# A four-layer convolution stack with state-space scan: group norms through a product, and logarithms written to PSUM

## The chip, the cores and the metric

The kernel runs on one core of a Trainium2 chip. A core has five engines with a queue each: TensorE (PE, with its weight loads shown as PEld), VectorE (DVE), ScalarE (ACT), GpSimd (POOL) and SyncE (SP), which here issues nearly all transfers. Each queue runs in order: an instruction that waits holds back everything behind it on its engine. The metric is the device time of one execution in microseconds (us), lower is better. Before the change it is 4212.91 us, the median of three runs (4212.07 to 4213.04).

## The reference: what is computed

Four images of 128 channels and 64 x 64 pixels (4096 positions) go through four layers. Each layer first normalises its input over groups (32 groups of 4 channels each) and adds its result to that input:

```
gn(v): per image and group of 4 channels:  (v - mean) / sqrt(var + 1e-5)
x = x + attention(gn(x))      # one head over 4096 positions, 128 channels, softmax
x = x + conv5x5(gn(x))        # weights built from radial tables
x = x + ssm(gn(x))            # 1x1 product, causal conv of 4 taps, silu; delta = softplus(...);
                              # 64 channels forward, 64 backward, 64 states each:
                              # h = exp(delta*A)*h + delta*x*B ; y = sum over states of h*C + D*x ; 1x1 product
x = x + conv3x3(gn(x))        # the offset branch of the reference has no effect on the result
```

A group's mean and variance are over 4 channels times 4096 positions, so they need a sum over positions (along a partition) and one over channels (across partitions).

## The kernel before, in words

Channels lie on the 128 partitions, positions along them. An image's positions are cut into 8 blocks of 512 (`MM`) and 4 chunks of 1024 (`CH`).

**The scan is the backbone.** `scan_core` walks 1024 ticks: 256 for each image (4 chunks, 2 directions, 16 sets of 4 states, 2 halves of the channels). A tick `i` has these steps, each on its engine:
- drive (POOL, L1502): `db = dx * br` for tick i+2, one of three buffers;
- decay (ACT, L1495): `da = exp(de * a)` for tick i+1, in PSUM;
- recur (DVE, L1512): the scan `h = da*h + db`, and for most ticks the product with the row `cr` (L1515) behind it;
- weigh (POOL, L1533): that product for the other ticks (`to_pool`);
- collect (PE, L1551): sums over states, eight products for every two ticks of a set, issued three ticks behind;
- keep (ACT, L1528): the last column, for the next chunk.

Rows are loaded from DRAM by SP for each tick. While images wait in other stages PSUM is cut "wide" (a decay of 1024 in one instruction, two buffers); while the operands of the next image are made it is "narrow" (two decays of 512, three buffers, and a bank for the product's use). `widen` makes the turn between two ticks.

**All else is background work.** `images()` is a chain of Python generators that issue the attention, the 5x5 convolution (`conv_pairs`), the scan's operands (`scan_prep`, `scan_operands`) of the next image, and the last 3x3 convolutions (`conv`, `conv_last`) of earlier ones. Every `yield` names a cost, and twice in each tick the main loop takes work until a credit, half a `pace` of `PACES`, is used up. So a yield is no wait on the chip: it sets how much is issued between two ticks' own instructions, and so the order in every queue. At an image's boundary `before(b)` issues background work without ticks until the next image's first operands are ready. Image 0's first three layers run before the scan begins, with nothing beside them; the last convolution of image 3 runs after it ends.

**Group norms.** In a layer's last step each block's sum comes out of the instruction that writes the block (`st.sum`), and ACT squares the block less one of its pixels with an accumulator (`Sums.squares`, L338). `group_norm` then makes scale and offset. For these sums it runs 13 small DVE instructions: `aggregate` (L345 to L348), a transpose within blocks of 32 that brings four channels beside each other (L366), means and variances of groups (L374 to L384), and a transpose back (L386). Then it waits, in the order of work, for the next tick, and POOL takes the power -1/2 and the offset (L391, L392). ACT applies them (`normalise`, L397). There are four such norms with bn_stats before the attentions (tag a, not changed), and twelve with sums: e before the 5x5 convolution, s before the scan's operands, m before the last convolution, one of each for each image.

**Attention's end.** For image 1 and later the last half block is evicted from PSUM (L736), inverted (DVE, L744), divided (ACT, L753), turned to channels (PE, L758 and L763), added (ACT, L768) and squared (L338), with yields between these steps.

**The operand stage.** `scan_operands` works in slots: for each block taps on PE, halves and tanh on ACT (L1270, L1277), silu on DVE (L1281), products on PE, and softplus as max(z, 0) + log(1 + exp(-|z|)). The logarithms come in two groups of four blocks (L1343)[...]; `join` adds each to `delta` (L1318), for the first group on POOL and for the second on DVE; `drives` multiplies on POOL (L1323).

Of the kernel before, what the change touches and what calls it, by code (L numbers as in the profile page):

```python
# [24 lines left out]
F32 = mybir.dt.float32  # L25
I32 = mybir.dt.int32
AF = mybir.ActivationFunctionType
# [5 lines left out]
P = 128  # L33
# [13 lines left out]
PACES = 2.65, 2.62, 2.62, 1.55  # L47
# [6 lines left out]
def conv_preact_kernel(  # L54
# [72 lines left out]
    gsz = C // GROUPS  # L127

# [191 lines left out]
    class Sums:  # L320
# [12 lines left out]
        def squares(self, i, x, pixel):  # L333
            if not self.begun:
                nc.scalar.activation(self.away, pixel, AF.Identity, scale=-1.0)
                self.begun = True
# [5 lines left out]
        def aggregate(self):  # L342

            total = gn_sums[:, 0, 0:2]
            nc.vector.tensor_reduce(total, self.sums, AX.X, ALU.add)  # L345
            nc.vector.tensor_scalar(gcols[:, :, 0], total, 1.0 / L, None, ALU.mult)
            nc.vector.tensor_tensor(self.away, gcols[:, 0, 0:1], self.away, ALU.add)
            nc.vector.scalar_tensor_tensor(  # L348
                gcols[:, 1, 0:1], self.away, self.away, gcols[:, 1, 0:1], ALU.mult, ALU.subtract
            )  # L350
# [3 lines left out]
    def group_norm(st, name):  # L354
# [5 lines left out]
        by_sums = isinstance(st, Sums)  # L360
        if by_sums:
            st.aggregate()
        else:
            nc.vector.bn_aggr(gcols[:, :, 0], st.rearrange("p a b -> p (a b)"))
# [15 lines left out]
        nc.vector.tensor_tensor(means, means, vars_, ALU.subtract if by_sums else ALU.add)  # L380
# [7 lines left out]
        begun = ticks_begun[0]  # L388
        while begun and ticks_begun[0] == begun:
            yield 0.4  # L390
# [98 lines left out]
    def attention_first(b, xs, xn, v, st, loads):  # L489
# [112 lines left out]
        def settle(blk):  # L602
# [6 lines left out]
            st.squares(blk, xs[:, cut], xs[:, 0:1])  # L609
# [50 lines left out]
    def attention(b, xs, xn, v, st, safe, loads):  # L660
# [94 lines left out]
        def turn(blk):  # L755
# [6 lines left out]
            for t in range(TPM):  # L762
# [6 lines left out]
                xs[:, cut], sums.pop(blk), AF.Identity, bias=bv_c, accum_out=st.sum(blk)  # L769
# [3 lines left out]
        def squares(blk):  # L773
            st.squares(blk, xs[:, bass.ts(blk, MM)], xs[:, 0:1])
# [51 lines left out]
        yield HOP / 2  # L826
        invert(done)
        divide(done)
        yield HOP
        turn(NM - 1)  # L830
        yield 2 * PRODUCT
        squares(NM - 1)
        ready.add((b, "attended"))


    def conv(b, xs, tag, st, weights, k, finish, name, residual=False):
# [10 lines left out]
        gn = yield from group_norm(st, f"{name}{b}")  # L847
# [46 lines left out]
    def conv_last(b, xs, st, finish):  # L894
# [5 lines left out]
        gn = yield from group_norm(st, f"m{b}")  # L900
# [98 lines left out]
    def conv_pairs(b, xs, tag, st, st2, lean):  # L999
# [9 lines left out]
        gn = yield from group_norm(st, f"e{b}")  # L1009
# [89 lines left out]
        def add(c, y, acc):  # L1099
# [5 lines left out]
            st2.squares(i, chunk(xs, c, y), xs[:, 0:1])  # L1105
# [97 lines left out]
        yield HOP  # L1203
        done()
        ready.update({(b, "convolved"), "narrow"})
        while "wide" in pools:
            yield HOP
# [4 lines left out]
    def scan_prep(b, xs, st, mats4):  # L1212
# [3 lines left out]
        pad = KC - 1  # L1216
# [705 lines left out]
```

## Time and profile before

| what | value |
|---|---|
| median of three runs | 4212.91 us |
| the profiled execution, and its span | 4214.73 us, 4212.9 us |
| DVE busy | 3581.9 us (85%), 2561 instructions |
| POOL busy | 3519.0 us (84%), 1679 instructions |
| PE busy | 3684.3 us (87%), ends modelled |
| ACT busy | 2334.0 us (55%) |
| mean granted TensorE clock | 0.931 |
| first drive of the scan, end of the scan | about 674 us, about 4144 us |
| a tick beside an attention | about 3.15 us |
| a tick in an operand stage | about 5 us |

The page gives, for each engine, busy time as a share of the span; a group of instructions has its line, engine and operation, the tensors it writes and reads, its count, its busy time, the mean of one, and the idle time in front of it with what ended that. A timeline row has its start and duration in us and, in brackets, the idle time of its engine before it. Ticks are numbered here by their drive (the instruction that writes `db`), 0 to 1023.

### The profile page before, as it was taken

How to read it: one execution, taken by the hardware profiler on the slowest of the kernel's cores; microseconds unless marked ns; L12 is line 12 of the kernel's file. 1: busy time of each engine (PE TensorE's matmuls, PEld its weight loads, DVE VectorE, ACT ScalarE, POOL GpSimd, SP SyncE). 2: the span in 40 equal slices, each digit the busy share in tenths (PEclk: the TensorE clock that was granted, in tenths of full speed). 3: DMA queues.
4: the chain of work that ended last, by engine and by line, in shares of the span. 5: the costliest groups of instructions: out<-in, count | busy, mean ns of one | idle time of the engine just before them, and what ended most of it. 6: DMA issues, size and time to landing. Idle time of an engine off the chain costs nothing. (4 is left out here: it accounts for less than half of the span.)

```text
span 4212.9 us, 49863 instructions
## 1 busy us (share of the span) xinstructions
PE 3684.3 (87%) x17628; PEld 2132.3 (51%) x17628; DVE 3581.9 (85%) x2561; ACT 2334.0 (55%) x3911; POOL 3519.0 (84%) x1679
## 2 busy tenths in 40 slices
PE   8999997999998979999989789999898476575766
PEld 4444443888884327887853268888633122121212
DVE  3842216999999989999999889999999899999995
ACT  3344316667674376776654666676645554545442
POOL 2533315999999978999999889999998899999995
PEclk9999999999999989999999989999999688786877
DMA  2120006555555566555555665555555666666561
GB/s 65 40 94 26 3 20 241 192 195 186 195 187 193 190 243 214 196 193 193 193 185 191 212 233 194 190 191 196 189 185 205 247 198 221 207 209 236 193 236 58
DMA packets 223728, 740.99 MB, mean 176 GB/s; under 512 B 29662, under 2 KB 30942, under 8 KB 223212
## 3 DMA queue, kind: packets, MB, share of 16 engines
q1 hardware_dynamic: 221548, 736.99, 51.8%
q8 instruction: 140, 2.29, 0.2%
q14 instruction: 120, 0.98, 0.1%
q10 hardware_dynamic: 1920, 0.73, 0.1%
HBM read 662.14 MB, written 75.47 MB: 175 GB/s over the span
## 5 line engine op out<-in xcount | busy, mean ns | idle before, releaser
L1502 POOL TENSOR_TENSOR db<-dx,br 128x1024 f32<-128x1024 f32 x1024 | 2400.5, 2368 | 133.6 <-DVE hc L1512 38.9
L1495 ACT ACTIVATE da<-de,a_neg 128x1024 f32<-128x1024 f32 (+1 forms) x1092 | 1161.7, 1065 | 400.4 <-DVE hc L1515 269.4
L1512 DVE TENSOR_TENSOR_SCAN da<-da,last,db 128x1024 f32<-128x1024 f32 (+1 forms) x501 | 1151.1, 2298 | 13.0 <-ACT da L1495 5.8
L1515 DVE TENSOR_TENSOR hc<-da,cr 128x1024 f32<-128x1024 f32 (+1 forms) x714 | 834.1, 1168 | 62.7 <-issue 0.9
L1551 PE MATMUL y<-hc,sel 128*32 128x512 f32 x4096 | 605.5, 653 | 268.1 <-POOL hc L1533 178.3
L1533 POOL TENSOR_TENSOR hc<-hc,cr 128x1024 f32<-128x1024 f32 x348 | 823.2, 2366 | 14.4 <-ACT last L1528 11.9
L700 PE MATMUL sc<-r,x 128*128 128x256 f32 x3072 | 803.6, 387 | 29.4 <-ACT last L1528 16.5
L721 PEld LDWEIGHTS acc<-v,exchange 128*128 128x128 f32 x6144 | 800.2, 192 | 46.5 <-issue 10.0
L721 PE MATMUL acc<-v,exchange 128*128 128x129 f32 x6144 | 803.5, 275 | 0.0
L700 PEld LDWEIGHTS sc<-r,x 128*128 128x128 f32 x3072 | 530.9, 192 | 191.9 <-ACT last L1528 69.9
L1512 DVE TENSOR_TENSOR_SCAN hc<-da,last,db 128x1024 f32<-128x1024 f32 (+1 forms) x267 | 596.0, 2232 | 0.9 <-ACT da L1495 0.9
L713 ACT ACTIVATE exchange<-sc 128x512 f32<-128x512 f32 x768 | 444.7, 589 | 216.8 <-PE sc L700 209.0
L1551 PEld LDWEIGHTS y<-hc,sel 128*32 128x32 f32 x4096 | 114.0, 113 | 623.0 <-POOL hc L1533 252.4
L1512 DVE TENSOR_TENSOR_SCAN da<-da,db 128x1024 f32<-128x1024 f32 (+1 forms) x175 | 381.4, 2179 | 24.4 <-ACT da L1495 17.2
L522 POOL TENSOR_TENSOR sidep<-sidep,exchange 128x512 f32<-128x512 f32 x120 | 172.5, 1437 | 245.4 <-ACT exchange L504 242.9
L1528 ACT COPY last<-da 128x1 f32<-128x1 f32 x516 | 81.1, 157 | 510.8 <-DVE hc L1515 510.0
L504 ACT ACTIVATE exchange<-sc 128x512 f32<-128x512 f32 x256 | 152.6, 596 | 253.7 <-PE sc L503 248.9
L522 DVE TENSOR_TENSOR sided<-sided,exchange 128x512 f32<-128x512 f32 x120 | 98.7, 822 | 211.4 <-ACT exchange L504 210.4
L510 PE MATMUL acc<-exchange,v 128*128 128x512 f32 x512 | 262.0, 594 | 0.9
L503 PE MATMUL sc<-r,x 128*128 128x512 f32 x512 | 262.0, 594 | 0.6 <-ACT r L486 0.6
L865 PE MATMUL pcm<-xpm,cs 128*128 128x512 f32 x432 | 214.3, 645 | 42.6 <-ACT xpm L397 42.6
L1512 DVE TENSOR_TENSOR_SCAN hc<-da,db 128x1024 f32<-128x1024 f32 (+1 forms) x81 | 181.4, 2240 | 1.6 <-ACT da L1495 1.4
(266 smaller groups left out, 3094.6 us busy)
## 6 DMA issues: line engine op xcount, KB each, us to landing
br<-bm SPq DMA_DIRECT2D x512, 512.0 KB, 3.9
cr<-cm SPq DMA_DIRECT2D x512, 512.0 KB, 4.5
dx<-dxd SPq DMA_DIRECT2D x64, 512.0 KB, 5.8
de<-dd SPq DMA_DIRECT2D x64, 512.0 KB, 6.0
xs<-in_x_dram SPq DMA_DIRECT2D x16, 512.0 KB, 6.2
xsd<-xs SPq DMA_DIRECT2D x16, 512.0 KB, 5.6
xcd<-xc SPq DMA_DIRECT2D x16, 512.0 KB, 2.7
bm<-bs SPq DMA_DIRECT2D x32, 256.0 KB, 4.1
```

The source lines that it names most:

```text
L503: nc.tensor.matmul(sc, xn[:, bass.ts(j, P)], rq[blk], start=True, stop=True)
L510: nc.tensor.matmul(acc[blk], v[:, j, :C], ring[:, u % NRING, :], start=j == 0, stop=j == NJT - 1)
L522: eng.tensor_tensor(s, s, ring[:, u % NRING, :], ALU.add)
L700: nc.tensor.matmul(sc[:, bass.ts(n, HM)], xn[:, bass.ts(2 * k + n, P)], rq[blk][:, cut], start=True, stop=True,)
L713: nc.scalar.activation(pt, sc, AF.Exp)
L721: nc.tensor.matmul(acc[part][:, bass.ts(t, CV)], ring[:, u % NRING, n * HM + t * P : n * HM + (t + 1) * P], v[:, 2 * k + n, :], start=(k, ...
L1495: nc.scalar.activation(da, rep["de", b, c, d, g][:, bass.ts(h, size)], AF.Exp, scale=a_neg[:, at(i)])
L1502: nc.gpsimd.tensor_tensor(dbs[i], rep["dx", b, c, d, g], rows["b", b, c, d, q], ALU.mult)
L1512: nc.vector.tensor_tensor_scan(h, da, db[:, cut], before, ALU.mult, ALU.add)
L1515: nc.vector.tensor_tensor(hc[:, cut], h, rows["c", b, c, d, q][:, cut], ALU.mult)
L1533: nc.gpsimd.tensor_tensor(hcs[i], hcs[i], rows["c", b, c, d, q], ALU.mult)
L1551: nc.tensor.matmul(y[r : r + SG, :], sel, hcs[first + gg][:, bass.ts(h, MM)], start=False, stop=q == NQ - 1, tile_position=(0, r), skip_gr ...
```

## The change

- **The norm's mean over channels** is made by PE. A constant matrix `gmean` has 1/(4 x 4096) within each group of four channels and zero elsewhere; it is made once from the identity by two DVE instructions. `Sums.settle` reduces the block sums to two numbers a channel, multiplies them by `gmean` into two columns of a PSUM bank that its caller has at hand (`spare`), and makes variance and negative mean with four small DVE instructions that read PSUM. POOL's power and offset stay. `group_norm` is kept for the norms before the attentions.
- **The pixel** that is taken off before squaring becomes the group's mean of that pixel, by a one-column product (e and m); the s norm takes the e norm's mean (`follow`).
- **The order of work.** The norm's POOL steps follow in the tick of the norm; the wait for the next tick is now in front of the e norm (`next_tick` after the attention's last squares) and inside the s norm (`wait`). The yields between the steps of the attention's end are gone, as is the one before the last add of the 5x5 convolution for images 1 to 3. `scan_prep` no longer waits for the wide PSUM tiles to go before its norm, but after its first two blocks.
- **Logarithms.** For images 1 to 3, the first three of the second group are written to PSUM banks ("a", "z", "s2"); the fourth stays in SBUF, and its add goes to POOL.
- **Paces** are 2.60, 2.57, 2.57 instead of 2.65, 2.62, 2.62; the last stays 1.55.

```diff
-PACES = 2.65, 2.62, 2.62, 1.55
+PACES = 2.60, 2.57, 2.57, 1.55
+    gmean = const.tile([P, P], F32, name="gmean")
+    gpick = const.tile([P, GROUPS], F32, name="gpick")
+    nc.vector.tensor_reduce(
+        gpick, ident.rearrange("p (g s) -> p g s", s=gsz), AX.X, ALU.add
+    )
+    nc.vector.tensor_scalar(
+        gmean.rearrange("p (g s) -> p g s", s=gsz),
+        gpick.unsqueeze(2).to_broadcast([P, GROUPS, gsz]), 1.0 / (gsz * L), None, ALU.mult,
+    )
...
-        def squares(self, i, x, pixel):
+        def squares(self, i, x, pixel, spare):
+
+            self.spare = spare
             if not self.begun:
-                nc.scalar.activation(self.away, pixel, AF.Identity, scale=-1.0)
+                nc.tensor.matmul(spare[:, 0:1], gmean, pixel, start=True, stop=True)
+                nc.scalar.activation(self.away, spare[:, 0:1], AF.Identity, scale=-float(L))
                 self.begun = True
...
+        def follow(self, other):
+
+            self.away, self.begun = other.minus, True
+
+        def settle(self, name, wait=False):
...
+            total = small.tile([P, 2], F32, tag="gn_total", name=f"total_{name}")
             nc.vector.tensor_reduce(total, self.sums, AX.X, ALU.add)
...
+            mean, power = self.spare[:, 0:1], self.spare[:, 1:2]
+            nc.tensor.matmul(self.spare[:, 0:2], gmean, total, start=True, stop=True)
...
+            nc.vector.tensor_scalar(off, mean, self.away, -1.0, ALU.add, ALU.mult)
+            nc.vector.scalar_tensor_tensor(less, mean, self.away, off, ALU.add, ALU.mult)
+            nc.vector.scalar_tensor_tensor(var, less, GN_EPS, power, ALU.add, ALU.add)
+            nc.vector.tensor_scalar(minus, mean, -1.0, None, ALU.mult)
+            if wait:
+                yield from next_tick()
+            nc.gpsimd.tensor_tensor(rs, var, mhalf, ALU.pow)
+            nc.gpsimd.tensor_tensor(nb, minus, rs, ALU.mult)
+            return rs, nb
+
+    def next_tick():
+
+        begun = ticks_begun[0]
+        while begun and ticks_begun[0] == begun:
+            yield 0.4
...
         def squares(blk):
-            st.squares(blk, xs[:, bass.ts(blk, MM)], xs[:, 0:1])
+            spare = sums.pop(blk)
+            if blk + 1 == NM:
+                spare = slots.take("sp")
+            st.squares(blk, xs[:, bass.ts(blk, MM)], xs[:, 0:1], spare)
...
         evict(done)
-        yield HOP / 2
         invert(done)
         divide(done)
-        yield HOP
         turn(NM - 1)
-        yield 2 * PRODUCT
         squares(NM - 1)
+        yield from next_tick()
         ready.add((b, "attended"))
...
-        gn = yield from group_norm(st, f"e{b}")
+        gn = yield from st.settle(f"e{b}")
+        st2.follow(st)
...
-        yield HOP
+        if not lean:
+            yield HOP
         done()
         ready.update({(b, "convolved"), "narrow"})
-        while "wide" in pools:
-            yield HOP
...
+        gn = yield from st.settle(f"s{b}", True)
         xn = pools["big"].tile([P, VSIZE], F32, tag="V", name=f"xn2_{b}")
         nc.gpsimd.memset(xn[:, :pad], 0.0)
         nc.gpsimd.memset(xn[:, pad + L : 2 * pad + L], 0.0)
-        gn = yield from group_norm(st, f"s{b}")
...
         piece(0)
         piece(NM - 1)
-        yield HOP
+        while "wide" in pools:
+            yield HOP
...
-                eng = nc.vector if b > 0 and c >= NCH // 2 else nc.gpsimd
+                eng = nc.vector if b > 0 and NM // 2 <= i < NM - 1 else nc.gpsimd
                 eng.tensor_tensor(delta[:, cut], delta[:, cut], us.pop(i), ALU.add)
...
             for n in range(i, j):
-                nc.scalar.activation(us[n], us[n], AF.Ln)
+                to = us[n]
+                if b > 0 and j == NM and n - i < 3:
+                    to = bank(("a", "z", "s2")[n - i], f"ln_{b}_{n}")
+                nc.scalar.activation(to, us[n], AF.Ln)
+                us[n] = to
```

More of the change, by code (lines that the diff above doesn't have):

```diff
@@ L340, in squares, with cell @@
             )
[L342 to L350, printed above, removed]
+        def follow(self, other):
+            self.away, self.begun = other.minus, True
+        def settle(self, name, wait=False):
+            def cell(tag):
+                return small.tile([P, 1], F32, tag=f"gn_{tag}", name=f"{tag}_{name}")
+            total = small.tile([P, 2], F32, tag="gn_total", name=f"total_{name}")
+            nc.vector.tensor_reduce(total, self.sums, AX.X, ALU.add)
+            mean, power = self.spare[:, 0:1], self.spare[:, 1:2]
+            nc.tensor.matmul(self.spare[:, 0:2], gmean, total, start=True, stop=True)
+            off, less, var, rs, nb = (cell(tag) for tag in ("off", "less", "var", "rs", "nb"))
+            minus = self.minus = small.tile([P, 1], F32, tag=f"gn_mi{name[0]}", name=f"mi_{name}")
+            nc.vector.tensor_scalar(off, mean, self.away, -1.0, ALU.add, ALU.mult)
[11 more added lines that the diff above has]
+            yield 0.4
     junk = const.tile([P, MM], mybir.dt.bfloat16, name="junk")
@@ L358, in tile @@
             return small.tile([P, *shape], F32, tag=f"gn_{tag}", name=f"{tag}_{name}")
[L360 to L364, printed above, removed]
+        nc.vector.bn_aggr(gcols[:, :, 0], st.rearrange("p a b -> p (a b)"))
         turned, after = gn_work[:, 0], gn_work[:, 1]
@@ L379, in group_norm @@
         nc.vector.tensor_tensor(means, means, means, ALU.mult)
-        nc.vector.tensor_tensor(means, means, vars_, ALU.subtract if by_sums else ALU.add)
+        nc.vector.tensor_tensor(means, means, vars_, ALU.add)
         total = gn_sums[:, 1]
@@ L387, in group_norm @@
         rs, nb = tile("rs", 1), tile("nb", 1)
-        begun = ticks_begun[0]
-        while begun and ticks_begun[0] == begun:
-            yield 0.4
         nc.gpsimd.tensor_tensor(rs, back[:, 0, 0:1], mhalf, ALU.pow)
@@ L608, in settle @@
             )
-            st.squares(blk, xs[:, cut], xs[:, 0:1])
+            st.squares(blk, xs[:, cut], xs[:, 0:1], pb)
         rq[0] = queries(b, 0, xn, slots)
@@ L768, in turn @@
             nc.scalar.activation(
-                xs[:, cut], sums.pop(blk), AF.Identity, bias=bv_c, accum_out=st.sum(blk)
+                xs[:, cut], sums[blk], AF.Identity, bias=bv_c, accum_out=st.sum(blk)
             )
@@ L846, in conv @@
         nc.gpsimd.memset(xp[:, pad : hp - pad, wp - pad :], 0.0)
-        gn = yield from group_norm(st, f"{name}{b}")
+        gn = yield from st.settle(f"{name}{b}")
         xh = xs.rearrange("p (h w) -> p h w", w=W)
@@ L899, in conv_last @@
         nc.gpsimd.memset(rows[:, H + 1, :], 0.0)
-        gn = yield from group_norm(st, f"m{b}")
+        gn = yield from st.settle(f"m{b}")
         xh = xs.rearrange("p (h w) -> p h w", w=W)
@@ L1104, in add @@
             )
-            st2.squares(i, chunk(xs, c, y), xs[:, 0:1])
+            st2.squares(i, chunk(xs, c, y), None, acc)
         def advance(c):
@@ L1633, in scan_end @@
             yield PRODUCT
-            st.squares(i, xs[:, cut], xs[:, i * MM : i * MM + 1])
+            st.squares(i, xs[:, cut], xs[:, i * MM : i * MM + 1], po)
     def program(safe):
```

## The prediction

> **What bounds the kernel now.** I read the page first, then the windows of time, the timelines of the group norms and of the end of an operand stage, the groups, and last the end of the chain.
>
> Windows: stretch, its length, then busy us (and count) of PE, PEld, DVE, ACT, POOL, then PE clock, DMA share, GB/s. The first lies in an attention, the second in an operand stage, the third in the last scan.
>
> ```profile
> 680.00:1280.00 600.00, 581.41 (x3944) 468.00 (x3941) 569.60 (x344) 419.59 (x755) 580.64 (x254) 0.99 0.59 197
> 1468.00:1593.00 125.00, 89.55 (x358) 35.20 (x351) 106.16 (x113) 88.70 (x149) 97.64 (x49) 0.84 0.70 242
> 3920.00:4140.00 220.00, 144.16 (x443) 41.38 (x446) 215.57 (x118) 96.63 (x117) 216.52 (x94) 0.77 0.61 207
> ```
>
> Outside the operand stages GpSimd (POOL) and VectorE (DVE) are both full. Per three ticks POOL has three drives and one weighing, 4 x 2.32 = 9.28 us, and DVE 3.5 + 3.5 + 2.3 = 9.3: a tick is 3.1 us, and neither engine has more than the buffered drives, some two ticks, in hand. Whatever stands idle on either here is paid. The operand stage is different: 24 ticks in 123 us, with no engine full.
>
> Next the group norm of image 2 before its last convolution (DVE, then POOL):
>
> ```profile
> 3886.06 2.34 DVE L1512 TENSOR_TENSOR_SCAN hc<-da,last,db 128x1024 f32<-128x1024 f32 x1
> 3889.06 0.17 DVE L345 TENSOR_REDUCE gn_sums<-su_m 128x2 f32<-128x16 f32 x1 [0.66 <-ACT junk L338]
> 3889.27 5.00 DVE L346 TENSOR_SCALAR gcols<-gn_sums 128x2 f32<-128x2 f32 x1
> ...
> 3896.58 0.25 DVE L386 STREAM_TRANSPOSE back_m<-gn_work 128x64 f32<-128x64 f32 x1
> 3896.75 2.32 DVE L1512 TENSOR_TENSOR_SCAN da<-da,last,db 128x1024 f32<-128x1024 f32 x1
> ```
> ```profile
> 3891.90 2.34 POOL L1533 TENSOR_TENSOR hc<-hc,cr 128x1024 f32<-128x1024 f32 x1
> 3896.91 0.55 POOL L391 TENSOR_TENSOR rs_m<-back_m,mhalf 128x1 f32<-128x1 f32 x1 [2.66 <-DVE back_m L386]
> 3897.54 0.19 POOL L392 TENSOR_TENSOR nb_m<-back_m,rs_m 128x1 f32<-128x1 f32 x1
> 3899.15 2.35 POOL L1502 TENSOR_TENSOR db<-dx,br 128x1024 f32<-128x1024 f32 x1 [1.43 <-DVE da L1512]
> ```
>
> The two-number L346 takes 5.00 us: it ends 0.03 us after POOL's weighing does. It, or L347 behind it, does so in nearly every norm beside the scan (0.17 us with POOL idle). So DVE loses 8.4 us, from 3888.40 to 3896.75, and then POOL idles.
>
> Last, the end of image 1's operand stage, and two groups:
>
> ```profile
> 1567.86 2.19 ACT L1343 ACTIVATE u<-u 128x512 f32<-128x512 f32 x4
> ```
> ```profile
> 1568.89 8.27 DVE L1318 TENSOR_TENSOR exchange<-exchange,u 128x512 f32<-128x512 f32 x4
> ```
> ```profile
> 1573.89 2.72 POOL L1323 TENSOR_TENSOR xc<-exchange,xc 128x1024 f32<-128x1024 f32 x1 [0.69 <-DVE exchange L1318]
> 1577.30 2.39 POOL L1323 TENSOR_TENSOR xc<-exchange,xc 128x1024 f32<-128x1024 f32 x1 [0.68 <-issue]
> 1580.43 2.35 POOL L1502 TENSOR_TENSOR db<-dx,br 128x1024 f32<-128x1024 f32 x1 [0.75 <-DVE da L1512]
> ```
> ```profile
> L1311 DVE TENSOR_TENSOR exchange<-exchange,pb 128x512 f32<-128x512 f32 x32 | 22.0, 687 | 1.1
> L1318 DVE TENSOR_TENSOR exchange<-exchange,u 128x512 f32<-128x512 f32 x12 | 21.0, 1802 | 0.3 <-ACT u L1343 0.3
> ```
>
> Four joins take 8.27 us: each reads two SBUF tiles while POOL works. L1311, the same add with one operand in PSUM, takes 0.69.
>
> **The change, part by part.** The sum is made against the profiled span, 4212.9 us (its execution took 4214.7; the median of the runs is 4212.91, so I take the differences off the median).
>
> *A norm's chain alone.* Thirteen DVE steps become a reduce, a product on PE and four cells; POOL's power waits for the third. Nothing runs beside it in image 0 (two norms before the scan) and at the very end. In the chain's end DVE steps run from 4153.90 to 4156.85 and POOL starts at 4156.92: 3.0 us. New: reduce 0.17; the product, which no row shows for two columns: from below the bare 128x1 product L587 (0.25), from above 1.0 (load 0.19, product, two hand-overs and a slow clock); taken 0.6, nearest to L587 with its load 0.19 and two hand-overs of 0.07; three cells at 0.21 (L348 0.22, L384 0.18). 1.4 us. Saved 1.6 x 3 = **4.7** (3.5 to 5.8). The second image-0 norm also moves two memsets behind the power; they had waited for nothing. gmean and gpick are made on DVE in its first idle 5.3 us: nothing; uncovered, 0.4.
>
> *Last-convolution norms, images 0 to 2* (beside the scan). Before, from drive start to drive start: ticks 798-800 took 14.45 against 9.4, ticks 871-876 25.27 against 18.8, ticks 945-950 26.28 against 18.8: 19.0 lost. After, the power stands in the norm's own tick. The cells read PSUM, so I give them no wait for POOL (the reduce, one SBUF input, never showed one); DVE stops 1.6 us, 2.6 where ACT's last squares stand in the same tick (image 1). POOL has memsets 0.35 and power and product 0.75, and waits up to 1.1. Lost: 1.4 + 2.6 + 1.7 = 5.7. Saved **13.3** (8 to 15).
>
> *Norms after attention, images 1 to 3.* Before: 9.2, 8.7 (without a 5.0 us tick that isn't its own) and 9.9 = 27.8. The removed steps of waiting put evict, reciprocal, divide, turn, xs and squares into one tick: on ACT 0.37 + wait 0.2 + 0.7 + wait 0.9 + 0.9 + 0.9 = 4 us, and the next tick's decay stands behind it; DVE has a scan of 2.3 or 3.5 in hand, so the decay (1.1 more) is about in time. But here POOL decides: memsets 0.6, power and product 0.75, memset 0.1, four differences 4.35, all now ahead of the next drive, and waits of 0.2 to 2.1 for the variance and 1.25 for ACT's first normalised piece: 9.0, 7.2, 7.2 = 23.4. Saved **4.4** (0 to 9): the shorter DVE chain is mostly covered by POOL's own work.
>
> *Operand stages, images 1 to 3.* (a) Logarithms to PSUM: three adds become 3 x 0.69, one goes to POOL (1.27, its row). DVE is free at 1571.0 instead of 1577.1. POOL: drives to 1572.8, add 1574.0, two products 1578.8, so the next drive starts at 1578.8 instead of 1580.43; the third scan after, which needs it, at 1581.15 instead of 1584.80: 3.65. Two rules of the skill bear here. "VectorE: DVE Perf Modes", Rules for kernel authors, says that an elementwise step on a PSUM source runs at 1x at best, and to copy to SBUF first if much is done with it: by it the PSUM operand gains nothing, and one more add on POOL costs 1.27 an image. "GPSIMD Engine Reference", Key points, says that the two engines contend where DVE has two SBUF inputs. The rows (0.69 against 1.80) side with the second; by the first the sum would be 3 x (3.65 + 1.27) = 15 us poorer. (b) The norm in front now starts in the tick of the convolution's last add, a tick or so sooner, and before the PSUM tiles turn narrow. By the built program's order (numbered by drive) the stage ends at 258, 513, 767 instead of 259, 514, 768, so one tick loses its cover: 3.5 less 1.15 that ACT saves, -2.35. ACT is the stage's dense engine (4.6 of 4.65 us in most of its ticks), and there is a new wait: the first narrow decay waits for the last wide scan, then six normalisings (6 x 0.75) stand ahead of its second half. DVE idles some 3.8 us, then 2.2 at the first silu. In this stage DVE already idles 13 us for ACT's results, so I take the stall as absorbed; if it isn't, it is 6.0 an image. (c) Operands are ready a tick sooner against the scan's fixed boundary, where ACT waited 3.74 us for de and POOL 2.39 for dx in image 1, POOL 5.28 in image 2, none in image 3; 0 to 3.7, taken 1.7. Together 3 x (3.65 - 2.35 + 1.7) = **9** (-9 to 22).
>
> *The rest, at nothing.* The first squares of six stages wait for a one-column product (0.5 us each, ACT 30% idle there; without that cover 3). Lower paces spread PE's work over 2% more ticks; the removed steps of waiting were paced too, so the stages begin and end within a few ticks of where they did. The bank of a last block is held until the cells have read it: its next writer stands behind the norm anyway. SP: xsd's four stores and the weights' loads go out a tick earlier or later, no new wait.
>
> Sum: 4.7 + 13.3 + 4.4 + 9 = 31.4. 4212.9 - 31.4 = **4181.5**, say 4182; its own range 4170 to 4194.
>
> **Rivals.**
> - *POOL hides it* (0.18). What DVE saves beside the scan is lost as POOL's waits, since POOL must still do its work. For it: POOL 96.8% busy in the attention window. Against: POOL's own 2.66 and 1.43 idle. Then 4.7 + half of the 13.3 + nothing from the other two = 11: 4202 (4196 to 4208).
> - *More than summed* (0.22). The DMA waits at the boundary go wholly (3.7 and 5.3), the DVE idle in the operand stage shrinks with its joins, and lower paces free ACT's waits for PE (65 us in 520 of attention): 20 to 25 more, 4159 (4148 to 4169).
> - *Slower* (0.06). The operand stage's hand-over: the 6.0 us DVE stall isn't absorbed, the uncovered tick costs 3.5 in full, and ACT, a tick behind, delivers the last logarithms late, so that the joins' 3.65 is lost as well and boundary loads go out 3 us later: 12.5 an image, 37.5 in all, against 22.4 elsewhere, 4228. It decides from 22.4 / 3 = 7.5 us an image. Against: ACT's work in the stage hardly grows.
> - *No measurable change* (0.06): POOL hides it and half a stall eats the rest: 4211.
>
> **How the numbers follow.** A measurement of this kernel can tell about 0.2%, 8.4 us: faster is under 4204.5, slower over 4221.3. The likeliest case has 0.48. Faster: 0.48 + 0.22 + two thirds of 0.18 = 0.82; same: the rest of 0.18, 0.06, and 0.01 of the slow case = 0.13; slower 0.05. The range 4156 to 4206 leaves out the lower end of the second rival and the two cases above it.
>
> **What would show it.** No norm cell over 0.3 us beside the scan, 1.4 us from reduce to power in image 0 and at the end, joins from PSUM near 0.7, ticks of the last-convolution norms 12 to 13 us shorter in sum, operand stages (ticks 240 to 266, 135 us) 3 us shorter. Wrong if cells that read PSUM still wait for POOL, if DVE idles more in the operand stage than the joins give back, or if POOL's idle moves to the first difference.

## The result

The changed kernel takes 4185.37 us (median of four runs, 4181.65 to 4187.66) beside 4212.49 us for the kernel before on the same chip: a ratio of 0.9938, 95% interval 0.9921 to 0.9955. That is 27 us faster. The profiled execution took 4187.43 us, its span 4184.1. The forecast was 4182.

Where the difference of the two profiled spans lies, in fixed ranges of ticks (drive to drive), beside the sum of the prediction. The two columns on the right belong to experiments told below: the new norms alone (E5), and the new norms with the logarithms (E10).

| stretch (ticks) | before, us | changed | predicted | E5 | E10 |
|---|---|---|---|---|---|
| image 0, to the first drive | 674.4 | -1.8 | -3.1 | -1.8 | -0.9 |
| e norms (184-196, 438-450, 693-705) | 143.6 | -3.4 | -4.4 | -9.4 | -9.8 |
| operand stages (240-300, 494-556, 749-784) | 652.0 | -9.6 | -9 | -10.9 | -22.4 |
| m norms (793-803, 864-882, 936-956) | 166.6 | -10.0 | -13.3 | -13.4 | -13.6 |
| behind the last drive | 75.9 | -3.2 | -1.6 | -2.1 | -2.4 |
| all other ticks | | -0.9 | 0 | -1.5 | -3.4 |
| span | 4212.9 | -28.9 | -31.4 | -39.1 | -52.5 |

("All other ticks" differ by some us from one execution to the next, so small differences of the spans say little.) The total came near the forecast. The columns on the right say that this was not for the predicted reasons alone: two parts of the change give 46 us by the timed runs, and the third, the new order of work, takes some 20 back.

First the windows of time of the changed kernel (columns as before: stretch, length, busy us and count of PE, PEld, DVE, ACT, POOL, clock, DMA share, GB/s), for an attention, an operand stage and the last scan:

```profile
680.00:1280.00 600.00, 576.19 (x3878) 461.00 (x3875) 568.61 (x344) 414.60 (x749) 581.21 (x254) 0.98 0.58 197
1466.00:1591.00 125.00, 94.76 (x409) 40.97 (x412) 92.88 (x97) 90.34 (x149) 99.06 (x50) 0.88 0.68 236
3894.00:4114.00 220.00, 134.90 (x431) 36.55 (x429) 215.22 (x118) 93.80 (x114) 216.52 (x94) 0.74 0.61 206
```

Attention and last scan look as before: DVE and POOL stay full. In the operand stage DVE's busy time fell from 106.2 to 92.9 us: the joins take 6 us less and the norm's small steps 4 us less. DVE waits more instead.

The timeline of the last-convolution norm of image 2 in the changed kernel, DVE, POOL and ACT:

```profile
3850.85 0.16 DVE L365 TENSOR_REDUCE total_m<-su_m 128x2 f32<-128x16 f32 x1
3851.69 0.22 DVE L370 TENSOR_SCALAR off_m<-po,aw_m 128x1 f32<-128x1 f32 x1 [0.68 <-PE po L367]
3851.95 0.22 DVE L371 SCALAR_TENSOR_TENSOR less_m<-po,aw_m,off_m 128x1 f32<-128x1 f32 x1
...
3852.34 2.35 DVE L1545 TENSOR_TENSOR_SCAN da<-da,last,db 128x1024 f32<-128x1024 f32 x1
...
3859.57 2.35 DVE L1545 TENSOR_TENSOR_SCAN hc<-da,last,db 128x1024 f32<-128x1024 f32 x1 [3.63 <-ACT last L1561]
```
```profile
3851.27 2.34 POOL L1566 TENSOR_TENSOR hc<-hc,cr 128x1024 f32<-128x1024 f32 x1
...
3853.92 0.55 POOL L376 TENSOR_TENSOR rs_m<-var_m,mhalf 128x1 f32<-128x1 f32 x1
...
3862.00 2.36 POOL L1535 TENSOR_TENSOR db<-dx,br 128x1024 f32<-128x1024 f32 x1 [2.65 <-DVE hc L1545]
```
```profile
3854.77 3.51 ACT L424 ACTIVATE xpm<-xt,nb_m,rs_m 128x1024 f32<-128x1024 f32 x3 [5.42 <-POOL nb_m L377]
3858.19 0.13 ACT L1561 COPY last<-da 128x1 f32<-128x1 f32 x1
3858.35 1.12 ACT L1528 ACTIVATE da<-de,a_neg 128x1024 f32<-128x1024 f32 x1
```

The cells take 0.22 us although POOL's weighing runs beside them. DVE is held 1.49 us, not 8.4. But the power stands in the norm's own tick now, and the three normalised pieces behind it (3.51 us on ACT) stand ahead of the `last` and the decay of the next tick. DVE waits 3.63 us for those, and POOL, two drives further on, waits 2.65 us for DVE. DVE has such a wait in five of the six norms e and m beside the scan: 2.05, 3.41, 3.41 (e) and 2.11, 3.63 us (m of images 0 and 2). Only m of image 1 has a decay between its pieces.

What such a wait costs is read from POOL. The ranges of the table run from drive to drive, and drives are POOL's. In the e and m ranges POOL's busy time is the same before and after within 0.3 us, so their length changes with POOL's idle time alone. In the m norms the delay reaches POOL: 2.65 us in image 2 and 1.39 in image 0. In the e norms it doesn't. There POOL has four differences to make before its next drive, and goes on to that drive without a wait. POOL in the e norm of image 2, where DVE waits 3.41 us up to 2168.78:

```profile
2163.13 0.55 POOL L376 TENSOR_TENSOR rs_e<-var_e,mhalf 128x1 f32<-128x1 f32 x1 [0.97 <-DVE mi_e L373]
...
2165.31 1.11 POOL L1051 TENSOR_TENSOR df<-xpe 128x528 f32<-128x528 f32 x1 [1.32 <-ACT xpe L424]
...
2169.60 4.65 POOL L1535 TENSOR_TENSOR db<-dx,br 128x1024 f32<-128x1024 f32 x2
```

So POOL idles for the variance (2.42, 0.97 and 3.03 us in images 1 to 3) and for ACT's first normalised piece (1.32 each). Before, it was 2.67, 2.46 and 3.39 us for the norm's result and 1.4 each for the scan behind it.

The chain's end, where nothing runs beside the norm, and the end of image 1's operand stage:

```profile
4127.86 0.17 DVE L365 TENSOR_REDUCE total_m<-su_m 128x2 f32<-128x16 f32 x1 [8.11 <-ACT junk L351]
4128.50 0.22 DVE L370 TENSOR_SCALAR off_m<-po,aw_m 128x1 f32<-128x1 f32 x1 [0.48 <-PE po L367]
...
4129.25 0.55 POOL L376 TENSOR_TENSOR rs_m<-var_m,mhalf 128x1 f32<-128x1 f32 x1 [10.47 <-DVE mi_m L373]
```
```profile
1568.53 1.64 ACT L1375 ACTIVATE ln<-u 128x512 f32<-128x512 f32 x3
...
1569.17 1.88 DVE L1347 TENSOR_TENSOR exchange<-exchange,ln 128x512 f32<-128x512 f32 x3 [7.13 <-ACT ln L1375]
```

From reduce to power it is 1.39 us (1.59 and 1.39 in image 0). Three joins take 1.88 us.

The beginning of the same stage, right behind the s norm (DVE, then ACT):

```profile
1481.83 1.23 DVE L1548 TENSOR_TENSOR hc<-da,cr 128x1024 f32<-128x1024 f32 x1
1483.94 1.28 DVE L1545 TENSOR_TENSOR_SCAN hc<-da,last,db 128x512 f32<-128x512 f32 x1 [0.89 <-ACT da L1528]
1488.70 1.28 DVE L1545 TENSOR_TENSOR_SCAN hc<-da,hc,db 128x512 f32<-128x512 f32 x1 [3.48 <-ACT da L1528]
```
```profile
1483.15 0.69 ACT L1528 ACTIVATE da<-de,a_neg 128x512 f32<-128x512 f32 x1 [5.23 <-DVE hc L1548]
1483.78 4.32 ACT L424 ACTIVATE xn<-xs,nb_s,rs_s 128x512 f32<-128x512 f32 x6
1488.00 0.67 ACT L1528 ACTIVATE da<-de,a_neg 128x512 f32<-128x512 f32 x1
```

This is the hand-over that the prediction described: the first narrow decay waits for the last wide scan, six normalisings come next, and DVE waits 3.48 us. The tick of the norm fell from 7.37 to 4.35 us, and the two behind it grew from 4.63 to 8.19 and from 2.46 to 5.70.

### The profile page after: what moved, and what is told of

Same layout as the page of the kernel before. It is cut to its first block, busy times and chain, and to the rows that moved or that the text cites. A ratio compares the mean times of both kernels' runs of the same rounds, so it can differ in the third digit from the quotient of the medians.

```text
span 4184.1 us, 49830 instructions
## 1 busy us (share of the span) xinstructions
PE 3687.0 (88%) x17668; PEld 2140.8 (51%) x17668; DVE 3514.0 (84%) x2441; ACT 2325.1 (56%) x3900; POOL 3525.7 (84%) x1688
## 5 line engine op out<-in xcount | busy, mean ns | idle before, releaser
L1548 DVE TENSOR_TENSOR hc<-da,cr 128x1024 f32<-128x1024 f32 (+1 forms) x698 | 824.7, 1182 | 61.8 <-issue 1.3
L1566 POOL TENSOR_TENSOR hc<-hc,cr 128x1024 f32<-128x1024 f32 x354 | 837.4, 2366 | 6.8 <-ACT last L1561 3.6
L1545 DVE TENSOR_TENSOR_SCAN hc<-da,db 128x1024 f32<-128x1024 f32 (+1 forms) x86 | 190.7, 2218 | 7.6 <-ACT da L1528 5.1
```

What stands on the lines that cost most here:

```text
L1545: nc.vector.tensor_tensor_scan(h, da, db[:, cut], before, ALU.mult, ALU.add)
L1548: nc.vector.tensor_tensor(hc[:, cut], h, rows["c", b, c, d, q][:, cut], ALU.mult)
L1566: nc.gpsimd.tensor_tensor(hcs[i], hcs[i], rows["c", b, c, d, q], ALU.mult)
```

## The experiments

Ratios are against the kernel before, run beside each on the same chip. E9 is the changed kernel once more. Line numbers in rows are those of each kernel.

| kernel | us | ratio, 95% interval |
|---|---|---|
| E1 logarithms back in SBUF | 4199.5 | 0.9975 (0.9965 to 0.9984) |
| E2 s norm behind the turn | 4172.3 | 0.9916 (0.9899 to 0.9932) |
| E3 pieces apart | 4172.3 | 0.9914 (0.9897 to 0.9930) |
| E4 cells read SBUF | 4192.7, one run | |
| E5 new norms alone | 4175.1 | 0.9922 (0.9905 to 0.9938) |
| E6 paces of before | 4179.4 | 0.9935 (0.9918 to 0.9952) |
| E7 = E2 + E3 + paces of before | 4151.1 | 0.9867 (0.9851 to 0.9884) |
| E8 = E3 + paces 2.62, 2.60, 2.60 | 4170.9 | 0.9916 (0.9899 to 0.9932) |
| E9 changed kernel again | 4184.2 | 0.9941 (0.9925 to 0.9958) |
| E10 new norms and logarithms alone | 4163.7 | 0.9894 (0.9878 to 0.9911) |
| E11 = E7 + products in PE's gaps, no pixel in image 0 | 4155.0 | 0.9867 (0.9851 to 0.9884) |
| E12 = E10 + paces 2.66, 2.63, 2.63 | 4162.3 | 0.9886 (0.9870 to 0.9903) |

**E1: the logarithms undone.**

```diff
-                eng = nc.vector if b > 0 and NM // 2 <= i < NM - 1 else nc.gpsimd
+                eng = nc.vector if b > 0 and c >= NCH // 2 else nc.gpsimd
...
-                    to = bank(("a", "z", "s2")[n - i], f"ln_{b}_{n}")
-                nc.scalar.activation(to, us[n], AF.Ln)
-                us[n] = to
+                nc.scalar.activation(us[n], us[n], AF.Ln)
```

> The changed kernel with one part undone: the logarithms of an operand stage's last group stay in SBUF, and all four joins of that group are on DVE again. If the joins set the end of the stage (step 4a), a join takes about 2 us again instead of 0.68, and each of the three stages is at least 3.65 us longer, 11 in all: about 4196. The two traces allow more, since from the stage's 13th tick to its 32nd the changed kernel gained 6.5, 9.7 and 6.0 us: up to 22, 4207, if the joins alone did that. Rival, the joins are hidden: DVE loses 6 us an image where it waits for ACT anyway, and the time stays at 4185 (4182 to 4188).

By the ratios it is 15 us slower than the changed kernel; the operand stages' ticks (the table's range) are 13.9 us longer, by image 9.5, 3.3 and 1.1. The joins set the end of the stage, as predicted, but far more in image 1 than in image 3. The groups of joins, min, median and longest of one in ns, first in the changed kernel, then in E1:

```profile
L1347 DVE TENSOR_TENSOR exchange<-exchange,ln x9: 661/679/686, 1569.2 to 3294.9; 128x512 f32<-128x512 f32 x9
```
```profile
L1347 DVE TENSOR_TENSOR exchange<-exchange,u x12: 666/952/7449, 1567.3 to 3308.6; 128x512 f32<-128x512 f32 x12
```

The same addition spreads from 0.67 to 7.45 us with both operands in SBUF, and from 0.66 to 0.69 with one in PSUM. Six of E1's twelve have a POOL instruction running beside them; these take 1.22 to 7.45 us, and each ends about 0.55 us behind the end of a POOL instruction. The other six, with POOL idle, take 0.67 to 0.69. In the changed kernel POOL runs beside all nine. The longest of E1 (DVE, then POOL) ends at 2443.73:

```profile
2436.28 7.45 DVE L1347 TENSOR_TENSOR exchange<-exchange,u 128x512 f32<-128x512 f32 x1 [0.63 <-ACT u L1372]
```
```profile
2436.22 2.35 POOL L1562 TENSOR_TENSOR hc<-hc,cr 128x1024 f32<-128x1024 f32 x1
2438.54 2.33 POOL L1531 TENSOR_TENSOR db<-dx,br 128x1024 f32<-128x1024 f32 x1
2440.84 2.35 POOL L1562 TENSOR_TENSOR hc<-hc,cr 128x1024 f32<-128x1024 f32 x1
```

What counts is not the speed of one addition by itself, which is the same, but whether POOL holds it up. In image 1 all four of E1's joins are held, in images 2 and 3 one each, which fits the uneven gain.

**E2: the s norm behind the turn to narrow tiles**, as in the kernel before.

```diff
-        if not lean:
-            yield HOP
+        yield HOP
         done()
         ready.update({(b, "convolved"), "narrow"})
+        while "wide" in pools:
+            yield HOP
...
-        gn = yield from st.settle(f"s{b}", True)
         xn = pools["big"].tile([P, VSIZE], F32, tag="V", name=f"xn2_{b}")
         nc.gpsimd.memset(xn[:, :pad], 0.0)
         nc.gpsimd.memset(xn[:, pad + L : 2 * pad + L], 0.0)
+        gn = yield from st.settle(f"s{b}", True)
+        yield HOP
...
         piece(NM - 1)
-        while "wide" in pools:
-            yield HOP
+        yield HOP
```

> The changed kernel with one part undone: the 5x5 convolution's last add, the s norm and the first two normalised blocks stand in the order of the kernel before, that is, the norm comes after the turn to narrow PSUM tiles. If the hand-over stall is paid (the prediction took it as absorbed): in the changed kernel the ticks 243 to 251, and their like in the other images, take 8.4, 6.7 and 8.9 us longer than before, with a DVE wait of 3.48 us in front of the second half of the first narrow scan. These go, less what the shorter norm had gained by not hiding the narrow decays: 4 to 7 us an image, 12 to 21 in all, 4164 to 4173. Rival, the stall is absorbed as predicted: 2.35 an image comes back and 1.7 of earlier operands is lost, 4183 (4180 to 4187).

The time is in the expected range, but not for the reason given. The stall at the stage's beginning is gone: ticks 243 to 249, with the norm now in 245, take 27.1 us instead of 39.5. Then most of it comes back at the boundary, where work is issued without ticks until the next image's first operands are ready; one tick takes 23.0 to 24.5 us in each image. POOL in that tick of image 1:

```profile
1519.67 2.37 POOL L1567 TENSOR_TENSOR hc<-hc,cr 128x1024 f32<-128x1024 f32 x1
1531.89 4.93 POOL L1348 TENSOR_TENSOR exchange<-exchange,u 128x512 f32<-128x512 f32 x4 [9.86 <-ACT u L1376]
```

By the table's ranges the stages are 4.0 us shorter than in the changed kernel, not 12 to 21. By the ratios the kernel is 9 us faster; the rest of that is spread over ticks that the edit doesn't touch and stays unexplained.

**E3: the pieces apart.** The e and m norms' pieces are issued one to a tick.

```diff
         piece(0)
-        yield HOP / 2
+        yield from next_tick()
         piece(1)
...
         differences(0)
+        yield from next_tick()
...
-            if i < 2:
-                piece(2 + i)
+            if i in (1, 3):
+                piece(2 + i // 2)
```

> The changed kernel with the normalised pieces of the e and m norms set apart: after the first piece of 1024 the next waits for the next tick, and so on, so that no three of them (3.5 us on ACT) stand ahead of a decay. For the e norm the differences on POOL move a tick with them. If ACT's pieces are what DVE waits for now: its waits of 2.05, 3.41, 3.41 (e) and 2.11, 0.23, 3.63 us (m) go, 14.8 in all, some of it taken up by POOL: 10 to 14 faster than the changed kernel, 4171 to 4175. Rival, POOL's own work decides in the e norms (step 3): only the 5.7 of m comes, 4180 (4177 to 4182). Rival, the later start of the convolutions costs what the waits gave: 4185.

Time as expected: by the ratios 10 us faster than the changed kernel. DVE's waits for ACT fell from 2.05, 3.41, 3.41 (e) and 2.11, 0.23, 3.63 (m) to at most 1.17 us in these ranges; the e ranges are 4.2 and the m ranges 3.4 us shorter than in the changed kernel, the rest lies in other ticks. In the m norms the gain is the one expected: POOL's 1.39 and 2.65 us behind DVE and ACT go. In the e norms it has another cause. The edit also sets a drive between the power and POOL's first difference, and what goes there is POOL's wait of 1.32 us for the first piece, in all three; the waits for the variance stay in images 1 and 3 (2.42 and 3.03). The rival that POOL's own work decides in the e norms failed by its time, 4180, but its mechanism is the one that the rows show.

**E4: cells that read SBUF.**

```diff
-            mean, power = self.spare[:, 0:1], self.spare[:, 1:2]
             nc.tensor.matmul(self.spare[:, 0:2], gmean, total, start=True, stop=True)
+            both = small.tile([P, 2], F32, tag="gn_both", name=f"both_{name}")
+            nc.vector.tensor_copy(both, self.spare[:, 0:2])
+            mean, power = both[:, 0:1], both[:, 1:2]
```

> The changed kernel with one instruction more in each norm with sums: the two product columns are copied to SBUF (about 0.2 us on DVE), and the four cells read the copy. If a small DVE instruction whose operands all lie in SBUF waits for POOL's running instruction, and one that reads PSUM doesn't, then at least one cell of each s norm beside the scan (POOL's drive ends about 1 us later) and of image 2's m norm (POOL's weighing ends 1.7 us later) takes 0.7 us or more, against 0.15 to 0.22 in the changed kernel. Norms with POOL idle (image 0, the end) keep cells of 0.15 to 0.25. Rival, the cells are short whatever they read: all between 0.15 and 0.25. The time tells little: 2.4 us more by the copies alone, up to 8 by the waits.

In image 2's m norm, DVE and then POOL:

```profile
3857.49 1.49 DVE L373 SCALAR_TENSOR_TENSOR less_m<-both_m,aw_m,off_m 128x1 f32<-128x1 f32 x1
```
```profile
3856.61 2.34 POOL L1568 TENSOR_TENSOR hc<-hc,cr 128x1024 f32<-128x1024 f32 x1
3858.89 0.16 POOL L873 MEMSET xpm<- 128x66 f32 x1
```

`less` ends with POOL's weighing, and in each of the three s norms beside the scan it takes 0.64 us up to the end of POOL's drive (0.70 was the line drawn; it stood nearer to the end of the drive than assumed). Elsewhere, with POOL idle, it takes 0.22. The copy, which reads PSUM, and `off`, which reads one SBUF column as a tensor, don't wait beside the same POOL instructions (0.16 and 0.21). (In the kernel before L346, which reads one SBUF tensor of two columns, did wait; one column against two was not tried apart. L347, with two SBUF columns, waited up to 2.26 us there.) So `less`, with two SBUF columns as tensor operands, waits, and in the changed kernel, where one of the two lies in PSUM, it takes 0.22 beside POOL's work in the same four norms. `var` reads two SBUF columns as well, but nothing of POOL's except memsets stood beside it; there it took 0.16. In the other eight norms POOL is idle at these cells. What the wait costs in time isn't shown: there is one run, and the copies add time of their own.

**E5: the new norms alone, and E10: the new norms and the logarithms.** E5 is the changed kernel with the order of before in the attention's end (its three yields), the paces of before, the edits of E1 and E2, and the m and e norms with the wait for the next tick ahead of POOL's power and a `HOP` behind it. E10 is the same without the edit of E1.

```diff
-        gn = yield from st.settle(f"e{b}")
+        gn = yield from st.settle(f"e{b}", True)
+        yield HOP
```

> The kernel before with one part of the change alone: the twelve norms with sums go through the product (and its mean of one pixel), but the order of work, the waits for the next tick, the paces and the logarithms are those of before. If the chain itself carries the first two steps: 4.7 at the norms alone, and in the m norms DVE stops 1.6 to 2.6 us instead of 5.3 to 8.4, so most of the 13.3 comes even with POOL's power in the next tick: 18 to 22 faster than the kernel before, about 4192 where before is 4212. The s norms give nothing, since the decays of the turn to narrow tiles had been hidden behind them, and the first products of a pixel cost 1.4 us in image 0. Rival, the order of POOL's power decides and the chain is covered by what else DVE and POOL wait for: 4.7 and 3, 4205.

> The kernel before with two parts of the change: the norms through the product, and the logarithms in PSUM; the order of work and the paces are those of before. If the parts add up, what the logarithms were worth in the changed kernel (14) comes on top of what the product alone gave: 4160 to 4164, some 20 faster than the whole change, so that the new order and paces cost about 20. Rival, the joins set the stage's end only where the norm stands ahead of the turn: the logarithms give 0 to 4 here, 4171 to 4175, and the order costs about 10.

> The changed kernel as it is, on the same chip as the next two, so that they are compared with it directly: 0.9938 of the kernel before again (0.992 to 0.9955), about 4183.

The product alone is 32 us faster than before, more than either expectation. The part not foreseen is the s norm: its tick falls from 7.37, 7.35 and 7.36 us to 3.57, 3.51 and 3.52, and in sum most of these 3.8 us stays (10.9 in the table's ranges), although the decays of the turn had been hidden behind that norm. By image it is 0.5, 6.1 and 4.3: in image 1 nearly all is lost again between ticks 255 and 266, and why was not traced. With the logarithms it is 4163.7, where the changed kernel on the same chip takes 4184.2: the parts add up, and the new order of work with its paces costs 20 us. By ranges, E10 against the changed kernel: operand stages 12.8, e norms 6.5, m norms 3.6 us. Why the waiting form is better is seen in image 2's m norm of E10 (ACT, then DVE):

```profile
3850.02 0.16 ACT L1567 COPY last<-da 128x1 f32<-128x1 f32 x1 [4.07 <-DVE hc L1554]
3850.21 1.12 ACT L1534 ACTIVATE da<-de,a_neg 128x1024 f32<-128x1024 f32 x1
3851.27 3.49 ACT L424 ACTIVATE xpm<-xt,nb_m,rs_m 128x1024 f32<-128x1024 f32 x3
3854.66 0.14 ACT L1567 COPY last<-da 128x1 f32<-128x1 f32 x1
```
```profile
3856.04 2.36 DVE L1551 TENSOR_TENSOR_SCAN da<-da,last,db 128x1024 f32<-128x1024 f32 x1 [0.27 <-ACT da L1534]
```

With the power one tick later ACT makes the next decay first and the three pieces behind it, in time in which DVE has a scan in hand: 0.27 us of wait instead of 3.63. And POOL, which comes to its power a tick later, finds the variance ready in eight of the nine norms beside the scan, and has a drive to do while ACT makes the first piece. In the e ranges its waits for variance and piece, 10.4 us in the changed kernel, come to 1.97 here, and those for the scan behind the norm to 1.9.

**E6, E8, E12: only the paces, or the place of the stages.**

```diff
-PACES = 2.60, 2.57, 2.57, 1.55
+PACES = 2.65, 2.62, 2.62, 1.55
```

> The changed kernel with the paces of before (2.65, 2.62, 2.62). The prediction put the paces at nothing: 4182 to 4188, like the changed kernel. By the built order the operand stages then begin at ticks 238, 488 and 738 instead of 243, 498 and 753, and their second half is ready 5, 10 and 16 ticks sooner. Rival, operands that lie ready before the boundary are worth something: waits for transfers and the long tick at the boundary go, 5 to 15 faster, 4170 to 4180. Rival, PE and ACT are more loaded beside the attention, so that ticks there wait: 5 slower.

> The changed kernel with the pieces apart and paces of 2.62, 2.60, 2.60: the operand stages begin at 242, 496 and 750, about where the changed kernel has them, with the norm ahead of the turn as there. If the pieces' 10 to 14 us were gained at the norms and not by the later begin of the stage: 4171 to 4175 again. If the long boundary tick of the kernel with the pieces apart (18.4, 17.1, 24.7 us) cost something, it is faster by 4 to 10 more: 4162 to 4170. Rival, the gain there came from the stage's place alone: 4182 to 4185.

> The kernel with the product and the logarithms alone, and paces of 2.66, 2.63, 2.63, so that its operand stages begin at ticks 241, 495 and 750 instead of 243, 498 and 753, as in the kernel with pieces apart that took 0.9867 of the time before. If that kernel's lead of 12 us over this one was the place of the operand stages (in windows around them it is 0.7, 4.0 and 3.7 us ahead), most of it comes: 0.988 of the kernel before, 4154 to 4158 where before is 4210. Rival, the lead came from the pieces set apart at the e and m norms: the time stays at 0.9894, 4163 to 4166.

None of the three moves the time beyond its interval: E6 against the changed kernel 0.9935 and 0.9938, E8 against E3 0.9916 and 0.9914, E12 against E10 0.9886 and 0.9894. (E6's 4179.4 us lies below its expected range, but the kernel before was 5 us faster on that chip too.) The paces are worth nothing that can be measured, as predicted, although they move a stage by up to 15 ticks; so the place of the operand stages isn't what sets these kernels apart.

**E7: both repairs together, and E11 on top of it.**

> The changed kernel with the pieces apart and the norm after the turn (both as in the two kernels before), and with the paces of before, so that the operand stages begin at ticks 241, 496 and 751 instead of 245, 501 and 757 and the first half of the operands is ready by the order at 251, 506 and 761, ahead of the boundary at 254, 509 and 764. If what the norm's late start gave was lost again at the boundary (a tick of 23 to 24.5 us in each image, where work is issued without ticks until operands are ready), that tick goes, and both gains stand: 20 to 28 faster than the changed kernel, 4157 to 4165. Rival, the stage is ACT's, and a stall taken from its start only moves: 4172, like each alone.

E7 is the fastest kernel: 4151.1 us, 0.9867 of before, by the ratios some 30 us below the changed kernel. It is faster than expected. Its operand stages are 31.7 us shorter than before, against 9.6 in the changed kernel; E2 and E3 alone had 13.5 and 10.4. E11, which holds both repairs, ran beside E10 on one chip: 4155.0 against 4163.7 us. The long boundary ticks of E2 (23.0 to 24.5 us) are gone, as expected: the longest tick of each stage takes 11.1, 14.8 and 13.0 us. Whether the paces did that, by starting the stage four to six ticks sooner, or the pieces isn't settled, since E2 was not run with the paces of before. A shorter boundary tick alone needn't be a gain: E8's paces took E3's from 18.4, 17.1 and 24.7 us to 15.2, 13.5 and 15.0, and the time stayed. The stage's place by itself, tried in E12 without the two repairs, gave nothing.

```diff
+            if name in ("e0", "s0", f"m{B - 1}"):
+                flat = len(self.x.shape) == 2
+                idle = self.spare if flat else self.spare.rearrange("p (h w) -> p h w", w=W)
+                for _ in range(5):
+                    nc.tensor.matmul(idle, gmean, self.x, start=True, stop=True)
...
+            if b == 0 and not safe:
+                nc.vector.memset(st.away, 0.0)
+                st.begun = True
```

> The kernel with pieces apart, the norm after the turn and the paces of before, and two things more where nothing runs beside a norm (image 0's e and s norms and image 3's m norm): five products of 512 columns, whose result nobody reads, stand behind the cells on PE; and in image 0 the number taken off before squaring is zero, so that no product of a pixel has to wait for DVE there. If PE's slow clock after an idle stretch (0.50 for the first 4 us of the products behind each of these norms, then 1.00) comes from the idle stretch, the products behind the three norms start at a clock near 1.00 and are up to 2 us shorter each; and the 1.4 us that PE and ACT lost at the first squares of image 0 come back: 4 to 7 us faster, 4144 to 4147. Rival, the clock after the norm is set by something else than PE's work in the gap: no products shorter, the extra ones delay the first by up to 1 us each: 4150 to 4152.

No gain: 0.9867 again. The pixel's part came (ACT is some 1 us earlier from the first squares on). For the clock, PE behind image 0's e norm, in the changed kernel and in E11:

```profile
495.52 0.59 PE L367 MATMUL pzb<-total_e,gmean 128*128 128x2 f32 x2 [2.75 <-DVE total_e L365]
500.25 6.99 PE L1148 MATMUL pq<-xpe,cs 128*128 128x512 f32 x10 [4.15 <-ACT xpe L424]
```
```profile
493.97 0.38 PE L367 MATMUL pzb<-total_e,gmean 128*128 128x2 f32 x2 [2.75 <-DVE total_e L365]
495.18 7.55 PE L378 MATMUL pzb<-xs,gmean 128*128 128x512 f32 x10 [0.82 <-DVE mi_e L373]
502.57 4.49 PE L1154 MATMUL pq<-xpe,cs 128*128 128x512 f32 x10
```

The first ten instructions of the convolution take 4.49 us instead of 6.99. The granted clock, 0.50 from 500 to 505 us in the changed kernel, is 1.00 from 502.5 to 507 in E11, so PE's work in the gap does set the clock behind it. But the five products run at the slow clock themselves (0.50 from 495 to 501), 7.55 us for a gap of 4.15: the convolution starts 8.6 instead of 4.7 us behind the norm's product, a greater loss than the 2.5 us saved.

## Why the prediction was right, and where it was not

The time, the sign and the range held; the sum of 31.4 measured 28.9. That the two are so close is luck in part: two of its four terms came out too high, and a third is right by errors that cancel. By its steps:

- **The chain alone**: right. 1.59, 1.39 and 1.39 us from reduce to power where 1.4 was said; 1.5 + 1.6 + 1.6 saved. Two terms were missing. At the end another 1.1 us came from PE: its first 24 instructions of the last convolution took 12.27 instead of 13.37 us, behind an idle stretch of 7.1 us, with the norm's small product in it, instead of 8.8. In image 0 the first squares' product, put at nothing, costs: PE stands in order behind DVE's result there, and the work from there on is up to 1.7 us late.
- **m norms**: the cells and DVE's stops of 1.5 to 2.2 us were right. The term that failed is what follows the power, put at nothing: "The power stands in the norm's own tick" also puts three pieces of 3.5 us ahead of the decay, and DVE waits 2.11 and 3.63 us. POOL idles 1.39 and 2.65 us for that, and waits 1.88 for the variance in image 1, where up to 1.1 was allowed. 10.0 instead of 13.3; with the power a tick later (E10) 13.6. Here moving the step early was a loss, not a gain.
- **e norms**: 3.4 measured, of which 1.7 is a tick (448, where POOL's drive waits for a transfer) that isn't the norm's, so 1.7 instead of 4.4. "Here POOL decides" was right; DVE's waits of 2.05 to 3.41 us, which the prediction didn't have, never reach POOL. So was the 1.25 for the first piece, measured 1.32. The term that was too small is the wait for the variance, "0.2 to 2.1": it took 2.42, 0.97 and 3.03. And "the shorter DVE chain is mostly covered by POOL's own work" holds only for a power in the norm's own tick. A tick later POOL's work covers the chain's time instead of adding to it, and E10 gains 9.8 (1.2 of it in tick 448).
- **Operand stages**: 9.6 against 9, by errors that cancel. (a) The joins were sized rightly in sum: 3 x 3.65 = 11 predicted, 11.5 (E5 to E10) and 13.9 (E1) measured. But the 3.65 was read from image 1 and taken for all three, and by image the two experiments give 8.0, -0.4, 3.9 and 9.5, 3.3, 1.1. Not every join is held: before, POOL holds three of the four in image 1 (the fourth takes 0.68 us) and two each in images 2 and 3. (b) "One tick loses its cover" counted the shorter s norm as worth nothing by itself; it is worth up to 3 x 3.8 = 11.4, 10.9 measured in sum. And "I take the stall as absorbed" failed: E10's stages, without the early norm, are 12.8 us shorter. The early norm, the stall and the boundary share that; E2, which undid the early norm alone, got 4.0 of it back. The rival of a slower kernel had named this mechanism and its threshold of 7.5 us an image; the price, some 4 an image on average (5.2, -1.0 and 8.6), stayed below it.
- **The rule on PSUM sources** against the one on contention: E1 and E4 side with the second, as the rows did.
- **The rivals**: "POOL hides it" describes the e norms of the changed kernel, but not the m norms; as a total it falls with the measured 27 us, and E5, where the shorter chain shows in every range, is against it and against "no change". "More than summed" was near what is there to be had, 46 us, but not by its terms (the paces gave nothing in E6), and the order of the same change took the surplus back.

## What to carry to other kernels

When a step is moved earlier, list what it releases on every engine, and what it must itself now wait for. Three normalisations that became ready one tick sooner stood ahead of the decay that DVE needed, and POOL, asked for its power sooner, stood idle until the variance came. An engine's wait costs only what it passes on to the engine that sets the pace: follow it there before it is put down as a loss. Try the parts of a change one by one even where the whole is faster; here two parts alone gave nearly twice the whole. Where two engines share SBUF, one operand in PSUM can be worth more for being undisturbed than for its speed.

## What the runs showed of the hardware that was not expected

- Whether a small DVE instruction waits for POOL's running instruction goes by its operands here: with two SBUF columns as tensors it took 1.49 us (0.64 in the s norms, E4), with one SBUF column (E4) or with one of the two in PSUM (changed kernel) 0.15 to 0.22 beside the same POOL instruction.
- A held DVE instruction isn't always let in when POOL's instruction ends. E1's join of 7.45 us outlasted three POOL instructions that followed each other without a gap, and in the kernel before L346 outlasted two in its 5.00 us; other joins were let in behind the first.
- After an idle stretch of these lengths PE's granted clock is low for some microseconds of work. The windows of the last convolution's beginning, before and changed (before, PE was idle for 8.8 us ahead of them; in the changed kernel for 7.1 us, with the norm's small product inside, the last 4.8 without a break):

```profile
4161.00:4165.00 4.00, 4.00 (x5) 1.80 (x6) 4.00 (x4) 0.33 (x1) 4.00 (x3) 0.50 0.00 0
4165.00:4169.00 4.00, 4.00 (x8) 1.62 (x7) 3.14 (x2) 0.00 (x0) 4.00 (x3) 0.77 0.00 0
4169.00:4175.00 6.00, 6.00 (x15) 2.66 (x14) 0.00 (x0) 0.63 (x2) 0.27 (x1) 1.00 0.00 0
```
```profile
4133.00:4137.00 4.00, 3.70 (x5) 1.67 (x6) 4.00 (x3) 0.66 (x1) 4.00 (x4) 0.50 0.02 4
4137.00:4141.00 4.00, 4.00 (x11) 1.81 (x10) 3.48 (x3) 0.00 (x0) 4.00 (x3) 1.00 0.00 0
```

The clock (third column from the end) is 0.50 in the first 4 us of both; in the next 4 it is 0.77 before and 1.00 in the changed kernel. Whether the shorter gap or the product inside it did that was not tried apart; E11 shows that PE's work inside a gap can.
